# Gate logits of the first 16 token tiles as dot products on VectorE, VectorE in written order in layer 0's last part, and weight loads by guess

## The chip, the cores and the metric

The kernel runs on one core of a Trainium2 chip. The metric is the device time of one execution in microseconds (us); a kernel's time is the median over its runs. The engines are TensorE (PE; its weight loads are listed as PEld), VectorE (DVE), ScalarE (ACT), GpSimd (POOL) and SyncE (SP), which here issues most of the DMA loads.

## The reference, cut to what matters

Two layers work on x of 2708 tokens by 256 features, with an adjacency matrix `adj` (2708 x 2708, about 1.2% ones). Each is an attention over neighbours, then a mixture of 8 experts. What the change touches is layer 0:

```python
# layer 0, attention
h = layernorm(x)
q, k, v = h @ Wq.T + bq, h @ Wk.T + bk, h @ Wv.T + bv
s = where(adj > 0, q @ k.T / sqrt(256), -9e15)
x = x + elu(softmax(s, axis=-1) @ v)
# layer 0, experts: 8 experts, the 2 best of each token
xt = layernorm(x)
logits = xt @ Wr + br                      # the gate: 256 -> 8
weights, top_idx = two best of softmax(logits), divided by their sum
xn = (xt - mean(xt)) * rsqrt(var(xt) + 1e-5)
for e in range(8):                          # hidden size 1024
    h_e = gelu((xn * ln_g[e] + ln_b[e]) @ W1[e] + b1[e])
    y_e = h_e @ W2[e] + b2[e]
x = x + sum over the two chosen experts of weights * y_e
```

Layer 1 has the same frame: an attention whose score is a sum of a source and a destination term, and experts of hidden size 512.

## The kernel before

**Tiles.** The tokens form 22 tiles of up to 128 (the last has 20 rows). As queries they are taken in six blocks: five of 512 (four tiles each) and a last one of 148 (two tiles, 20 and 21). Blocks are numbered 0 to 5.

**Attention of layer 0.** For each block the kernel goes through the 22 key tiles. For a key tile it makes `scores` (L545 two matmuls per half of the features into PSUM, L557 the exponential on ScalarE, L560 a VectorE operation that takes the minimum with a large number and multiplies by the mask). Three key tiles later (`LAG`) `attend` (L609) multiplies the masked exponentials with the values into four PSUM accumulators, one for each query tile. The last two key tiles (from `KEYS` = 20 on) lie in columns of `adj` that are treated apart: one more matmul with `apart` (L552) makes the score of non-neighbours hugely negative, and a VectorE comparison writes the mask. `apart` is loaded and compared by `load_apart` (the comparison is L432): at key tile 14 of each block, at key tile 0 in the last.

**Masks.** While block b is computed, `masks_of(b + 1)` makes the next block's masks step by step: loads of `adj` into a ring of three buffers, 20 conversions to one byte (L411) and 20 transposes of four-byte words (L417), both on VectorE.

**Routing.** When a block's accumulators are complete, `evict` copies them out and puts one generator per tile into a `Line`. At each key tile `line.step()` starts the next waiting generator if at least `gap` = 3 steps have passed since the last one, and moves all running generators one step. A generator is `finish` (the division by the sum, elu, addition of x) and then `Experts.route`: statistics (L251 to L257, with a power on GpSimd in L257), two normalisations (L261; `xt` for the gate, and the row for the expert, which is normalised twice), two transposes of `xt` on TensorE (L274) and their copy on ScalarE (L275), the gate matmuls (L1156), the bias, the two best, two small matmuls that count how many earlier tokens chose each expert (L1188, L1189), and two indirect DMA writes on GpSimd (L1207) that put the row into the list of each of its experts, in DRAM. Tiles 0 to 3 are so routed during block 1, and so on; tiles 16 to 19 during block 5 and after it.

**Experts of layer 0.** At key tile 5 of block 5, `open` makes a ring of four tiles for expert weights (1.15 MB each), and `begin` cuts the lists as they are after 16 tiles into chunks of 128 rows (`place`), then starts the row loads of three chunks (SP, L1387 and L1393) and the weight loads of three chunks (GpSimd, indirect, L1368; a row index far outside means that nothing is loaded, which is used where a ring tile already holds the expert). `run` goes through 45 chunks, called slots, in written code and through the rest in conditional code. A slot turns its rows (`turned`: VectorE, L1429 a transpose in blocks, L1435 scale and shift), multiplies up (L1457) with the GELU on ScalarE (L1465), and down (L1473); VectorE weights the result (`y`, L1479), and an indirect DMA adds it to the tokens.

**Order.** SP's queue is in written order in the whole kernel. In layer 0, TensorE, VectorE, ScalarE and GpSimd are ordered by a scheduler when the program is built; `issue_after(self.issued.ins)` keeps some VectorE work of the experts behind a given instruction. Layer 1's attention and experts have TensorE, ScalarE and VectorE in written order.

## Time and profile before

| | |
|---|---|
| runs of the kernel before | 1213.34, 1210.01, 1208.46 us; median 1210.01 |
| the profiled execution | 1217.16 us, of which the span of the profile is 1215.5 us |
| instructions | 20794 |
| busy: TensorE matmuls, its weight loads | 1145.4 us (94%), 924.1 us (76%) |
| busy: VectorE, ScalarE, GpSimd | 566.2 us (47%), 431.9 us (36%), 416.0 us (34%) |
| mean granted clock of TensorE | 0.982 of full speed |
| DMA | 197.11 MB, 162 GB/s in the mean |

An L and a number name the line of the kernel's file from which an instruction comes. A group of instructions is written as output<-inputs with the partitions and elements of one instruction; a duration is the time of one instruction on its engine, and since neighbours overlap at their ends, the time from one start to the next is often shorter. "Waits" put an engine's idle time down to the instruction of another engine that came last. The granted clock is the share of its full speed at which TensorE ran in a stretch. The span is measured in one execution, and the difference of 1.7 us to that execution's time lies around it.

### The profile page before, as it was taken

How to read it: one execution, taken by the hardware profiler on the slowest of the kernel's cores; microseconds unless marked ns; L12 is line 12 of the kernel's file. 1: busy time of each engine (PE TensorE's matmuls, PEld its weight loads, DVE VectorE, ACT ScalarE, POOL GpSimd, SP SyncE). 2: the span in 40 equal slices, each digit the busy share in tenths (PEclk: the TensorE clock that was granted, in tenths of full speed). 3: DMA queues.
4: the chain of work that ended last, by engine and by line, in shares of the span. 5: the costliest groups of instructions: out<-in, count | busy, mean ns of one | idle time of the engine just before them, and what ended most of it. 6: DMA issues, size and time to landing. Idle time of an engine off the chain costs nothing. (4 is left out here: it accounts for less than half of the span.)

```text
span 1215.5 us, 20794 instructions
## 1 busy us (share of the span) xinstructions
PE 1145.4 (94%) x6512; PEld 924.1 (76%) x6512; DVE 566.2 (47%) x2147; ACT 431.9 (36%) x1252; POOL 416.0 (34%) x519
## 2 busy tenths in 40 slices
PE   8989999999998999999999999998999988899990
PEld 5666666666665666789999999996999977789880
DVE  5466663754645647452222222224866776322224
ACT  3222221221212222353333333333776747444440
POOL 3011021110211213253333343334645558555540
PEclk9999999999998999899999999999999999999996
DMA  9394962999969394847677955633002427555557
GB/s 200 58 181 76 194 160 88 226 209 267 221 133 219 83 192 164 276 102 219 174 222 228 352 118 154 179 95 100 1 1 76 178 62 209 168 139 132 170 179 282
DMA packets 199628, 197.11 MB, mean 162 GB/s; under 512 B 91403, under 2 KB 183012, under 8 KB 193368
## 3 DMA queue, kind: packets, MB, share of 16 engines
q1 hardware_dynamic: 172442, 109.39, 40.6%
q0 software_dynamic: 26176, 83.56, 21.8%
q10 hardware_dynamic: 894, 2.77, 0.6%
q8 instruction: 54, 0.88, 0.3%
q14 instruction: 62, 0.51, 0.1%
HBM read 252.62 MB, written 66.15 MB: 262 GB/s over the span
## 5 line engine op out<-in xcount | busy, mean ns | idle before, releaser
L1457 PEld LDWEIGHTS mm<-xe,ring 128*128 128x128 f32 x2192 | 259.7, 194 | 26.0 <-issue 11.7
L1457 PE MATMUL mm<-xe,ring 128*128 128x128 f32 x2192 | 265.6, 278 | 14.5 <-DMA ring<-L_ffn_packed,weight_row 7.1
L1473 PE MATMUL acc<-ring,hT 128*128 128x256 f32 x1096 | 254.3, 381 | 1.1 <-issue 1.1
L1465 ACT ACTIVATE hT<-mm,ring 128x128 f32<-128x128 f32 x548 | 156.6, 370 | 273.1 <-issue 168.1
L1473 PEld LDWEIGHTS acc<-ring,hT 128*128 128x128 f32 x1096 | 201.3, 191 | 26.0 <-issue 2.3
L609 PEld LDWEIGHTS acc<-v,p 128*128 128x128 f32 (+1 forms) x880 | 159.7, 190 | 65.2 <-issue 41.0
L609 PE MATMUL acc<-v,p 128*128 128x257 f32 (+1 forms) x880 | 204.6, 384 | 2.3 <-DVE p L560 1.3
L545 PE MATMUL s<-g,xnT 128*128 128x512 f32 x420 | 203.0, 603 | 0.0
L1479 DVE SCALAR_TENSOR_TENSOR y<-acc,who,bias 128x256 f32<-128x256 f32 x92 | 44.4, 482 | 339.2 <-PE acc L1473 322.9
L257 POOL TENSOR_TENSOR ln_rs<-ln_rs,minus_half 128x2 f32<-128x2 f32 x88 | 66.0, 752 | 252.0 <-DVE ln_rs L253 214.4
L1207 POOL DMA_INDIRECT disp<-row,to x88 | 90.4, 1027 | 166.2 <-DVE to L1204 58.2
L1368 POOL DMA_INDIRECT ring<-L_ffn_packed,weight_row x92 | 97.6, 1060 | 128.3 <-PE acc L1473 88.4
L557 ACT ACTIVATE p<-s 128x512 f32<-128x512 f32 x105 | 62.5, 596 | 181.4 <-PE s L545 143.0
L854 PE MATMUL acc<-parts,m 128*128 128x266 f32 x924 | 126.2, 293 | 0.0
L854 PEld LDWEIGHTS acc<-parts,m 128*128 128x128 f32 x924 | 117.1, 185 | 4.1 <-ACT raw L881 0.9
L545 PEld LDWEIGHTS s<-g,xnT 128*128 128x128 f32 x420 | 76.6, 192 | 53.8 <-issue 50.5
L560 DVE SCALAR_TENSOR_TENSOR p<-p,mT 128x512 f32<-128x512 f32 x100 | 68.4, 686 | 95.2 <-ACT p L557 93.6
L1492 POOL DMA_INDIRECT xd<-y,who x45 | 71.8, 1595 | 118.7 <-issue 70.4
L821 ACT CAST m<-mT 128x512 fp32r<-128x512 fp8e4 (+4 forms) x168 | 71.6, 475 | 11.4 <-PE acc L854 7.0
L1485 POOL DMA_INDIRECT xd<-y,who x47 | 47.1, 1002 | 23.6 <-issue 11.0
L411 DVE TENSOR_SCALAR m_rows<-adj 128x512 fp8e4<-128x512 int32 (+1 forms) x105 | 42.1, 432 | 2.0 <-DMA adj<-in_adj_dram 1.9
L417 DVE STREAM_TRANSPOSE mT<-m_rows 128x128 int32<-128x128 int32 x100 | 33.4, 393 | 0.1
(252 smaller groups left out, 1028.3 us busy)
## 6 DMA issues: line engine op xcount, KB each, us to landing
adj<-in_adj_dram SPq DMA_DIRECT2D x100, 256.0 KB
L_ffn_packed<-in_L_ffn_W_dram SPq DMA_DIRECT2D x16, 1024.0 KB
xg<-disp SPq DMA_DIRECT2D x368, 32.0 KB
L_ffn_packed<-in_L_ffn_W_dram SPq DMA_DIRECT2D x16, 512.0 KB
neighbours<-mT SPq DMA_DIRECT2D x5, 1408.0 KB
mT<-neighbours SPq DMA_DIRECT2D x5, 1408.0 KB
xin<-in_x_dram SPq DMA_DIRECT2D x42, 128.0 KB
ring<-L_ffn_packed SPq DMA_DIRECT2D x4, 1154.0 KB
```

The source lines that it names most:

```text
L257: nc.gpsimd.tensor_tensor(rs[:r, 1], rs[:r, 0], minus_half[:r], ALU.pow)
L545: nc.tensor.matmul(ps[:kr, :nb], xnT[:, c, k0 : k0 + kr], g[:, c, :nb], start=(c == 0), stop=(c == DC - 1 and k < KEYS),)
L560: nc.vector.scalar_tensor_tensor(p, p, LARGEST, mask, op0=ALU.min, op1=ALU.mult)
L609: nc.tensor.matmul(accs[j][:r], p[keys, q0 : q0 + r], v[keys, k, :], start=(k == 0), stop=(k == NT - 1),)
L821: nc.scalar.copy(m[:, : q1 - q0], MASKS[b].of_key(mTs[b], k)[:, q0 - b * BN : q1 - b * BN],)
L854: nc.tensor.matmul(acc[:r], masks[t], parts[:, k, i], start=(k == 0 and i == 0), stop=False,)
L1207: nc.gpsimd.indirect_dma_start(disp[:], bass.IndirectOffsetOnAxis(ap=to[:r, j : j + 1], axis=0), rows2[:r, j], None,)
L1368: nc.gpsimd.indirect_dma_start(w, None, packed[:], bass.IndirectOffsetOnAxis(ap=self.weight_row[:, s : s + 1], axis=0), bounds_check=E * P ...
L1457: nc.tensor.matmul(ps[:, i, :], w[:, c * hidden + f * P : c * hidden + (f + 1) * P], xe[:, c, :], start=(c == 0), stop=(c == DC - 1),)
L1465: nc.scalar.activation(hT[:, f, :], ps[:, i, :], AF.Gelu, bias=w[:, b1 + f : b1 + f + 1])
L1473: nc.tensor.matmul(ps, hT[:, f, :], w[:, w2 + f * D : w2 + (f + 1) * D], start=(f == 0), stop=(f == hc - 1),)
L1492: start = nc.gpsimd.indirect_dma_start(xd[:], at, y, None, bounds_check=N - 1, oob_is_err=False, compute_op=ALU.add)
```

## The change

The diff has six parts. Line numbers change; a name says which line is meant.

1. *Gate by dot products.* `gate_rows` copies the gate's weights Wr to all 128 partitions, subtracts each expert's mean over the features and leaves them as `wr_rows` (8 rows of 256 in each partition). It runs once, in block 0 at key tile 18, with one of the three `adj` buffers as the place for the raw weights. `gate_dots` computes the eight logits of a tile as eight VectorE operations that multiply two 128 x 256 tensors and sum along the row: four in `route`'s first step, four in its second. The result is multiplied by the row's factor `once` and the bias is added. That holds for tiles 0 to 15 (`t < self.early`), which then have no normalised `xt`, no transposes and no gate matmuls. Tiles 16 to 21 keep the matmuls; their transposed copy now takes a `raw` buffer.
2. *The far columns.* `load_apart` only loads now, at key tile 4 of blocks 0 to 4, and for block 5 at key tile 18 of block 4; `compare_apart` makes the comparison where `load_apart` stood.
3. *Written order.* From the start of block 5 until the experts of layer 0 end, VectorE's instructions are in written order. In block 5 a tile's generator starts four steps after the one before (`line.gap = GROUP`).
4. *The ring by guess.* At key tile 5 of block 5 the first three ring tiles are loaded by SP with the weights of experts 0, 1 and 3, before it is known which experts the first slots need. `place` compares the guess with the experts found, and the indirect loads bring only what differs. The steps of `begin` (chunk lists, row loads, weight loads) are spread: six at key tile 5, one each at 12, 16 and 20.
5. *Rows turned a slot ahead.* `turned(s + 1)` is written after `up(s)` in layer 0 too; `issue_after` is gone.
6. *Buffers.* The pool `fold` is replaced by one buffer of the masks' ring; some tiles of `fold_gate` (layer 1's gate, made in block 1) come from another pool.

```diff
-    def fold_gate():
+    def fold_gate(pool):
+        wdst_b = pool.tile([P, D], F32, name="wdst_b", bufs=1)
+        nc.sync.dma_start(wdst_b, a["L1_gnn_w_att"][D : 2 * D].partition_broadcast(P))
         for c in range(DC):
-            junk = small.tile([P, D], F32, name="junk", bufs=1)
+            junk = pool.tile([P, D], F32, name="junk", bufs=1)
             nc.vector.scalar_tensor_tensor(
...
             )
-        share = routing.tile([P, DC, P], F32, name="gT", bufs=2)
+        share = pool.tile([P, DC, P], F32, name="gT", bufs=2)
         nc.gpsimd.memset(share[:, 0], 1.0 / D)
...
+    def gate_rows(raw):
+        raw = raw.rearrange("p (d e) -> p d e", e=E)
+        mean = small.tile([P, E], F32, name="gate_mean", bufs=1)
+        nc.vector.tensor_reduce(mean, raw.rearrange("p d e -> p e d"), AX.X, ALU.add)
+        nc.vector.tensor_scalar(mean, mean, 1.0 / D, None, ALU.mult)
+        nc.gpsimd.tensor_tensor(
+            wr_rows, raw.rearrange("p d e -> p e d"),
+            mean.unsqueeze(2).to_broadcast([P, E, D]), ALU.subtract,
+        )
+    def gate_dots(lg, x, r, experts, unused):
+        for e in experts:
+            nc.vector.scalar_tensor_tensor(
+                unused, x, 1.0, wr_rows[:r, e],
+                op0=ALU.mult, op1=ALU.mult, accum_out=lg[:r, e : e + 1],
+            )
...
                         nc.sync.dma_start(adj[: ROWS[t], j], rest[j * P : j * P + ROWS[t]])
-                nc.vector.tensor_scalar(
-                    apart, adj[:, :n], 0, None, ALU.is_le, saturate=False
-                )
+                return apart, adj[:, :n]
+            def compare_apart(apart, adj):
+                nc.vector.tensor_scalar(apart, adj, 0, None, ALU.is_le, saturate=False)
                 return apart
...
-            with tc.tile_pool(name="fold", bufs=1, side="right") as fold:
-                wq = load_dmajor(fold, "L0_gnn_Wq", D)
-                wk = load_dmajor(fold, "L0_gnn_Wk", D)
+            fold = wide.tile([P, MASKS[0].width], FP8, name="mT", bufs=3)
+            fold = fold[:, : 16 * DC * D].bitcast(F32).rearrange("p (i c n) -> p i c n", i=4, c=DC)
+            if True:
+                wq = load_dmajor(fold[:, 0], "L0_gnn_Wq")
+                wk = load_dmajor(fold[:, 1], "L0_gnn_Wk")
                 load_x(0)
                 load_x(1)
-                wv = load_dmajor(wide, "L0_gnn_Wv", D)
+                wv = load_dmajor(wide.tile([P, DC, D], F32, name="wv"), "L0_gnn_Wv")
                 for t in range(2, 9):
...
                     raw = rows.tile([P, VALUES + 1], F32, name="raw", bufs=6)
-                    copied = (nc.scalar.copy if j % 2 else nc.vector.tensor_copy)(
+                    (nc.scalar.copy if j % 2 else nc.vector.tensor_copy)(
                         raw[: ROWS[t], : D + 1], accs[j][: ROWS[t]]
                     )
-                    if j == 0:
-                        experts0.issued = copied
                     line.add(finish(t, raw, total))
...
             late, total, accs, apart = [], None, None, None
-            folding = fold_gate()
+            folding = fold_gate(wide)
             for b, (b0, nb, ts_) in enumerate(BLOCKS):
                 later_mask = iter(())
+                if b == last:
+                    line.gap = GROUP
+                    order0.enter_context(
+                        tc.manual_schedule(engines={mybir.EngineType.DVE})
+                    )
                 if b + 1 < len(BLOCKS):
...
                         load_x(ts_[j])
+                    if b < last and k == GROUP:
+                        apart_adj = load_apart(b)
                     if k == (0 if b == last else NT - 8):
-                        apart = load_apart(b)
+                        apart = compare_apart(*apart_adj)
+                    if b == last - 1 and k == NT - 4:
+                        apart_adj = load_apart(last)
                     late.append((b, k, scores(b, k, g, apart, mT)))
...
                         total = all_sum(wide, sums, wv, D, "total0")
+                    if b == 0 and k == NT - 4:
+                        raw = wide.tile([P, BN // QUARTER, P], I32, name="adj", bufs=3)
+                        raw = raw.rearrange("p n e -> p (n e)").bitcast(F32)
+                        nc.sync.dma_start(
+                            raw, a["L0_ffn_Wr"].rearrange("d e -> (d e)").partition_broadcast(P)
+                        )
+                        gate_rows(raw)
                     if k == NT - 6 and b + 1 < len(BLOCKS):
...
                     if b == last and k == LAG + 2:
-                        experts0.open()
-                        for _ in experts0.begin():
-                            pass
+                        n = FULL_AFTER[experts0.early]
+                        guess0 = experts0.open(
+                            [i * (n // RING) * E // (n + GROUP) for i in range(AHEAD)] + [-1]
+                        )
+                        for _ in range(AHEAD):
+                            next(guess0)
+                        begin0 = experts0.begin()
+                        for _ in range(6):
+                            next(begin0)
+                    if b == last and k in (LAG + 7, LAG + 11, LAG + 15):
+                        next(begin0)
                 nc.sync.dma_start(neighbours[b][:], mT)
...
             own_norm, xd, disp, seen = self.own_norm, self.xd, self.disp, self.seen
-            w_gate, gate_bias = self.w_gate, self.gate_bias
+            gate_bias = self.gate_bias
             r = ROWS[t]
...
             mean, once, twice, _ = norm_stats(x[:r], r)
+            lg = small.tile([P, E], F32, name="lg")
+            by_dots = own_norm and t < self.early
+            if by_dots:
+                dots = small.tile([P, E], F32, name="dots")
+                gate_dots(dots, x[:r], r, range(E // 2), rows2[:r, 1, :D])
+                logits = dots[:r]
             yield
...
             if own_norm:
-                xt = rows.tile([P, D], F32, name="xn", bufs=4)[:r]
-                normed(xt, x[:r], mean, once)
                 normed(by_quarters(rows2[:r, 0, :D]), in_chunks(x[:r]), mean, twice)
+                if not by_dots:
+                    xt = rows.tile([P, D], F32, name="xn", bufs=4)[:r]
+                    normed(xt, x[:r], mean, once)
             else:
...
             if own_norm:
+                if by_dots:
+                    gate_dots(dots, x[:r], r, range(E // 2, E), rows2[:r, 1, :D])
                 nc.vector.tensor_copy(rows2[:r, 1, :D], rows2[:r, 0, :D])
...
                 )
-            lg = small.tile([P, E], F32, name="lg")
             if logits is None:
-                gT = routing.tile([P, DC, P], F32, name="gT", bufs=2)
+                gT = rows.tile([P, VALUES + 1], F32, name="raw", bufs=6)
+                gT = gT[:, :D].rearrange("p (c n) -> p c n", c=DC)
                 to_columns(gT[:, :, :r], xt, r)
...
                     nc.tensor.matmul(
-                        ps[:r, :E], gT[:, c, :r], w_gate[:, c, :],
+                        ps[:r, :E], gT[:, c, :r], wr[:, c, :],
                         start=(c == 0), stop=(c == DC - 1),
...
             self.weights = []
+            if self.own_norm:
+                yield
             for s in range(AHEAD):
...
-                nc.scalar.copy(self.ring[i][:, :1], pace()[:, :1])
+                if pace:
+                    nc.scalar.copy(self.ring[i][:, :1], pace()[:, :1])
                 nc.sync.dma_start(self.ring[i], self.packed_weights[0][e * P : (e + 1) * P, :])
...
                 raw = two.tile([P, DC, P], F32, name="xe_raw") if own_norm else xe
-                with tc.issue_after(self.issued.ins) if own_norm and s < often else ExitStack():
-                    nc.vector.transpose(
-                        raw.rearrange("p c (t i) -> p t c i", t=GROUP),
-                        xg.rearrange("p t (c j) -> p t c j", c=DC),
-                    )
+                nc.vector.transpose(
+                    raw.rearrange("p c (t i) -> p t c i", t=GROUP),
+                    xg.rearrange("p t (c j) -> p t c j", c=DC),
+                )
                 if own_norm:
...
-            def up(w, xe, factor, gated):
+            def up(w, xe, factor):
...
                 if own_norm:
-                    with tc.issue_after(self.issued.ins) if gated else ExitStack():
-                        nc.vector.tensor_scalar(bias2, w[:, b2:b1], factor, None, ALU.mult)
+                    nc.vector.tensor_scalar(bias2, w[:, b2:b1], factor, None, ALU.mult)
                 else:
...
                 w, (_, who) = self.weights[s], self.rows_[s]
-                if own_norm:
-                    xe = turned(s)
                 after = turned(1) if s == 0 and not own_norm else None
-                hT, bias2 = up(w, xe, who[:, 1:2], own_norm and s < 2)
-                if s + 1 < s1 and not own_norm:
+                hT, bias2 = up(w, xe, who[:, 1:2])
+                if s + 1 < s1:
                     xe = after or turned(s + 1)
...
                 nonlocal behind, xe
-                if not own_norm:
-                    xe = turned(s0)
+                xe = turned(s0)
                 for s in range(s0, s1):
...
         experts0.run(line)
+        order0.close()
         early_rows.close()
...
```

More of the change, by code (lines that the diff above doesn't have):

```diff
@@ L188, in adj_ffn_kernel, with load_dmajor @@
     bfc_b = load_bcast("L1_gnn_b_fc", D)
-    wdst_b = load_bcast("L1_gnn_w_att", D, D)
-    def load_dmajor(pool, name, n):
-        t = pool.tile([P, DC, n], F32, name=f"{name}_w")
+    def load_dmajor(t, name):
         nc.sync.dma_start(t, a[name].rearrange("(c p) n -> p c n", p=P))
@@ L197, in adj_ffn_kernel @@
     wr = const.tile([P, DC, E], F32, name="wr")
+    wr_rows = rows0.tile([P, E, D], F32, name="wr_rows", bufs=1)
     wg = const.tile([P, DC, E], F32, name="wg")
@@ L229, in times_gate @@
         def times_gate(dst, src):
-            turned = routing.tile([P, DC, P], F32, name="gT", bufs=2)
+            turned = pool.tile([P, DC, P], F32, name="gT", bufs=2)
             to_columns(turned, src, P)
@@ L498, in layer0_attention @@
                 for w in (wq, wk):
-                    f = fold.tile([P, DC, D], F32, name=f"flat{len(flat)}")
+                    f = fold[:, 2 + len(flat)]
                     for o in range(DC):
@@ L1038, in adj_ffn_kernel, with __init__ @@
     class Experts:
-        def __init__(self, layer, hidden, packed_weights, w_gate, gate_bias, own_norm, xd, disp, early):
+        def __init__(self, layer, hidden, packed_weights, gate_bias, own_norm, xd, disp, early):
             self.hidden, self.packed_weights, self.own_norm = hidden, packed_weights, own_norm
-            self.w_gate, self.gate_bias, self.xd, self.disp = w_gate, gate_bias, xd, disp
+            self.gate_bias, self.xd, self.disp = gate_bias, xd, disp
             self.seen = const.tile([P, E], BF16, name=f"seen{layer}")
@@ L1478, in down @@
                 y = two.tile([P, D], F32, name="y", bufs=3)
-                self.issued = nc.vector.scalar_tensor_tensor(
+                nc.vector.scalar_tensor_tensor(
                     y, ps, who[:, 1:2], bias2, op0=ALU.mult, op1=ALU.add
@@ L1585, in adj_ffn_kernel @@
     packed1 = pack_weights("L1_ffn", 512, False)
-    experts0 = Experts(0, 1024, packed0, wr, br_b, True, xd0, disps[0], 16)
-    experts1 = Experts(1, 512, packed1, wg, gb_b, False, xd1, disps[1], 14)
+    experts0 = Experts(0, 1024, packed0, br_b, True, xd0, disps[0], 16)
+    experts1 = Experts(1, 512, packed1, gb_b, False, xd1, disps[1], 14)
     neighbours = [
@@ L1592, in adj_ffn_kernel @@
     line = Line(3)
+    order0 = ExitStack()
     layer0_attention(line)
```

## The prediction

> **What bounds the kernel now.** I read the page first, then TensorE's waits, the timeline at its longest stall, and the groups by shape. TensorE's row says who is full:
>
> ```profile
> PE 1145.4 (94%) x6512; PEld 924.1 (76%) x6512; DVE 566.2 (47%) x2147; ACT 431.9 (36%) x1252; POOL 416.0 (34%) x519
> ```
>
> A saved microsecond of TensorE work counts wherever TensorE doesn't wait. Layer 0's attention fills 0 to 501 us, its experts 502 to 829. The waits of TensorE up to 550 us (us in total, times, longest) add up to under 18 us:
>
> ```profile
> PE misc L466 <- ACT xnT L275: 3.2, 6, 0.7
> PE s L552 <- DVE apart L432: 3.0, 1, 3.0
> PE misc L274 <- DVE xn L261: 2.7, 6, 0.8
> PE acc L609 <- DVE p L560: 1.3, 1, 1.3
> ```
>
> The second is the one long stall. Its cost doesn't end with the 3.0 us; in the table of stretches the granted clock (after the counts) falls behind it:
>
> ```profile
> 370.00:375.00 5.00, 2.53 (x12) 1.88 (x10) 5.00 (x15) 0.00 (x0) 3.24 (x4) 1.00 1.12 197
> 375.00:380.00 5.00, 3.97 (x13) 2.24 (x14) 1.39 (x4) 0.77 (x2) 0.18 (x1) 0.55 1.07 274
> 380.00:385.00 5.00, 5.00 (x13) 2.66 (x12) 1.36 (x2) 1.20 (x2) 0.00 (x0) 0.77 0.98 338
> 500.00:505.00 5.00, 4.02 (x19) 3.48 (x19) 3.25 (x12) 0.74 (x2) 0.00 (x0) 0.68 0.93 323
> 505.00:510.00 5.00, 5.00 (x31) 4.89 (x31) 3.36 (x24) 3.07 (x9) 0.00 (x0) 0.64 0.52 169
> ```
>
> 0.55 and 0.77 over 10 us mean half clock for 6.8 us; the last two rows say the same at the experts' start. What gate logits cost TensorE is read from starts in its timeline:
>
> ```profile
> 225.89 1.90 PE L609 MATMUL acc<-v,p 128*128 128x257 f32 x8
> 227.62 0.38 PE L274 MATMUL misc<-ident,xn 128*128 128x128 f32 x2
> 227.84 1.88 PE L545 MATMUL s<-g,xnT 128*128 128x512 f32 x4
> 229.56 1.90 PE L609 MATMUL acc<-v,p 128*128 128x257 f32 x8
> 231.29 0.51 PE L1156 MATMUL misc<-wr,gT 128*128 128x8 f32 x4
> 231.66 1.96 PE L545 MATMUL s<-g,xnT 128*128 128x512 f32 x4
> 233.46 1.90 PE L609 MATMUL acc<-v,p 128*128 128x257 f32 x8
> ```
>
> One key tile is 1.73 (scores) + 1.72 (attend) = 3.45 us. The transposes add 0.22; the gate matmuls 0.37, and the scores after them last 1.80 instead of 1.72. One tile's gate: 0.67 us.
>
> **The Trainium skill.** "TensorE: Matmul & The Clock Gate", What's actually happening: one idle window of about 3.4 us halves the clock until a busy window has passed. The trace agrees: 3.02 us idle, then 6.8 us (two such windows) at half; it also shows 2.5 us idle enough at 836 and 1 us at 500, where the matmuls before were narrow. "SBUF — State Buffer", SBUF: two separate sides: a VectorE operation with two SBUF inputs and a GpSimd operation reading SBUF exclude each other. The dots have two such inputs; no row of this trace isolates that price.
>
> **Part 1, dots instead of matmuls.** Removed: 16 tiles (0 to 15, routed in blocks 1 to 4) x 0.67 = 10.7 us of TensorE, 16 ScalarE copies, 16 VectorE normalisations. Added: 128 dots. The nearest row is L212, the same shape with an accumulator (starts at 36.0 and 36.5, before anything competes):
>
> ```profile
> L212 DVE SCALAR_TENSOR_TENSOR junk<-wfc,L_gnn_w_att_b x2: 417/420/424, 36.0 to 36.5; 128x256 f32<-128x256 f32 x2
> L212 DVE DVE_READ_ACCUMULATOR junk<-wfc,L_gnn_w_att_b x2: 81/82/82, 36.3 to 36.8; 128x1 f32 x2
> ```
>
> "VectorE: DVE Perf Modes", the errata section, gives (N+151)/0.96 ns for fp32 with two tensors: 424 ns at 256, as here. Operations overlap at their ends: from the start of one dot to the next's is 0.457, to another operation's 0.35. I take 0.41; ends 0.35 and 0.46. 128 x 0.41 = 52 us, less 16 x 0.33 of normalisation: +47 us of VectorE over 335 us.
>
> Does it reach TensorE? The changed program's order gives the VectorE work between one mask multiply and the next; priced start to start (mask multiply 0.60, conversion 0.335, word transpose 0.24, 256-wide operations 0.20 to 0.40, narrow ones 0.08) block 1's key tiles 3 to 13 cost 3.5, 4.3, 3.7, 3.4, 4.0, 4.5, 3.4, 4.1, 3.5, 4.1, 3.4 = 41.9 us against 11 x 3.45 = 38.0. VectorE ends 3.9 us behind (5.4 at 0.46 a dot). The attend stands three key tiles after its scores: 10.35 us, less about 1.5 for exponential and multiply, leaves 8.85. So nothing is lost in block 1; block 2 ends 2.6 behind, block 3 at most 4.4. Only in block 4 are two tiles bunched after key tile 14: 11.6 us of VectorE before the next multiply, and TensorE's order wants the first tile's selection (L1188 now) 9.5 us after those scores, while VectorE gives it after 1.4 + 8.9 + 0.5 = 10.8. With the smaller waits that follow: -2 us. Filling the rows of weights (a reduction, 5.5 us on GpSimd if L764's 0.74 us for 256 is scaled by 8, a 1 MB broadcast) lies at block 0's end, where the DMA engines idle (105 to 120 us) and nothing needs it for four key tiles; it borrows one of three adjacency buffers, of which the mask loads have that slack.
>
> **Part 2, the far-column comparison (L432) split from its load.** Before, it stood behind eight conversions and eight transposes. Now, in block 3, after the last multiply come four of each: 4 x 0.335 + 4 x 0.24 + 0.34 + 0.36 = 3.0, plus 1.4 = 4.4 us after scores 19; TensorE arrives after 3 x 1.73 = 5.2. In block 4 it is ready 4 us early. The stall goes: +3.0 and half of 6.8 us of clock, together +6.4. The loads move on SP: one 0.3 MB load in small pieces now competes in block 0 at key tile 4, where the DMA share is 1.2: -1 (0 to -2).
>
> **Part 3, the last block in written order.** From TensorE's last comparison of block 4 to the end of attention took 452.8 to 500.7 = 47.9 us, 44.5 when the two attends (3.4) that the new order puts earlier are taken off. Following both queues: VectorE gives tile 15's selection and the first multiply about 11.0 us after that comparison, TensorE wants it at 9.7 (-1.3); then TensorE's queue has tile 16's transposes behind half an attend, and they wait for exponential, addition, statistics, the GpSimd power (0.75) and the normalisation in one chain until 17.1, TensorE being there at 14.1 (-3.0); later waits 2.5, TensorE's slack being used up. The end comes at 49.3, so -4.8. In this lie 1.3 us of gates of tiles 18 and 19, which before stood among the experts.
>
> **Part 4, the experts' start.** Before, slot 0 began at 501.7 and slot 5 at 542.7: 41.0 us for five slots of 7.03 (35.2), so 5.8 lost to four tiles' gates, half clock and inputs coming late (on SP, `xg` loads sat in a queue full of GpSimd's ring loads from 490 to 506). Now the ring's three direct loads (3 x 1.15 MB) are on SP at key tile 5, and from the reference's inputs the full chunks per expert after 16 tiles are 4, 4, 3, 4, 4, 3, 3, 4: slots 0, 1, 2 belong to experts 0, 1, 3, the guess, so GpSimd's three loads are skipped. Turned rows are ready a slot ahead. Left: two gates 1.3 and one half-clock window 1.7: 3.0, gain +2.8 (0 to +4.5). Queued behind the fills on SP are the row loads; they have 25 us. Steady slots don't change: TensorE has no gap there. VectorE's y now stands behind the next slot's turning, which has 7 us to spare. Layer 1's own order is unchanged.
>
> **Sum.** 10.7 + 6.4 + 2.8 - 2 - 4.8 - 1 = 12.1 us: the span 1215.5 becomes 1203.4. The profiled execution took 1217.2, 7 above the median of 1210.0; I move the median by the same: 1198.
>
> **Rivals.** (a) VectorE nowhere reaches TensorE in the last block and the experts start at full clock: 10.7 + 6.4 + 4.5 - 1.3 = 20, 1190. For it: TensorE waited for VectorE's multiply only 1.3 us before. Against: the chain of tile 16 is in written order. (b) Gains eaten: stalls of 1 to 3 us in blocks 1, 2 and 4, and the 3.0 us stall of part 3 falling into one clock window (-1.7 each): 1203 to 1209. For it: eleven key tiles in a row have more VectorE work than TensorE work. (c) Slower: VectorE becomes the bound in blocks 1 to 4, because a dot interleaved with GpSimd costs more than L212's. Block 1's lag is 3.9 + 32 x (price - 0.41), and TensorE stalls by what exceeds 8.85, four times; the 12 us are gone at 0.66 us a dot, and at 0.8 the four blocks lose 30, which gives 1228. Against it: L624, also two inputs, means 0.416 among GpSimd's work. (d) The guess doing nothing changes part 4 by at most its 2.8.
>
> **Chances.** Forecast 0.54 (its own range 1192 to 1204), (a) 0.10, (b) 0.21, (c) 0.15. About 0.5%, 6 us, is what can be told from no change here. Faster: forecast, (a) and a quarter of (b), 0.69; same 0.15; slower 0.16. The range 1188 to 1212 leaves out most of (c) and the lower tail of (a).
>
> **What would show it.** Right: 32 transposes gone from L274 and the gate matmuls down to six tiles; no 3 us gap before the comparison in block 3; TensorE gapless in blocks 1 and 2; small gaps near key tile 17 of block 4 and tile 16's transposes; slot 5 under 39 us after slot 0. Wrong: many gaps before attends ended by VectorE, dots above 0.5 us start to start, half-clock windows in blocks 1 to 4, or later mask conversions waiting for adjacency loads.

## The result and the profile after

The changed kernel takes 1230.3 us (median of six runs, 1227.1 to 1231.4), the kernel before 1210.7 us in the same comparison: a ratio of 1.0155 (95% interval 1.0137 to 1.0174). It is 19 us slower; 12 us faster was forecast. Its profiled execution took 1230.8 us, with a span of 1229.1.

The page's row of busy times after the change says that TensorE does less, as it should (96 matmul records and 6 us fewer), and VectorE 55 us more:

```profile
PE 1139.2 (93%) x6416; PEld 919.0 (75%) x6416; DVE 621.2 (51%) x2389; ACT 423.9 (34%) x1234; POOL 422.6 (34%) x524
```

So the loss is waiting. TensorE's waits over the whole changed kernel (us in total, times, longest) show where; the far-column stall of block 3 is gone from the list, and a six times longer one has come:

```profile
PE acc L632 <- DVE p_last L583: 21.3, 4, 17.9
PE mm L1512 <- DMA ring<-L_ffn_packed,weight_row: 8.9, 5, 3.1
PE misc L1242 <- DVE sel L1237: 5.1, 4, 2.1
```

The landmarks place it. They are the starts of the first matmul of a kind in the timeline, the end of the last attend, and the start of the last of 45 `y` of layer 0's written slots, all in us:

| | before | changed | difference |
|---|---|---|---|
| block 5 begins (first `g_last` scores) | 457.2 | 443.8 | -13.4 |
| attention ends | 500.7 | 521.0 | block 5: +33.7 |
| experts begin (first L1457, now L1512) | 501.7 | 522.7 | |
| `y` of slot 9 | 583.4 | 598.6 | from the attention's end: -5.0 |
| `y` of slot 44 | 826.1 | 841.8 | from slot 9: +0.4 |
| end of the span | 1215.5 | 1229.1 | from slot 44: -2.0 |

Up to block 5 and from the experts on the change does what was forecast, or more. Block 5, the smallest block, takes 77.2 us instead of 43.5. Its stretches (busy time of PE, PEld, DVE, ACT, POOL, then granted clock, DMA share and GB/s) are of the changed kernel:

```profile
445.00:450.00 5.00, 5.00 (x36) 4.15 (x35) 4.22 (x21) 1.47 (x5) 0.83 (x1) 1.00 1.00 237
450.00:455.00 5.00, 0.74 (x6) 0.46 (x5) 2.67 (x18) 0.83 (x4) 1.03 (x1) 0.79 1.07 225
455.00:460.00 5.00, 0.00 (x0) 0.00 (x0) 0.00 (x0) 0.00 (x0) 0.99 (x2) 0.50 1.18 155
460.00:465.00 5.00, 0.00 (x0) 0.00 (x0) 0.00 (x0) 0.00 (x0) 0.00 (x0) 0.50 1.08 200
465.00:470.00 5.00, 0.00 (x0) 0.00 (x0) 0.21 (x1) 0.00 (x0) 0.00 (x0) 0.50 0.71 168
470.00:475.00 5.00, 4.53 (x9) 1.58 (x10) 4.50 (x17) 0.79 (x3) 0.00 (x0) 0.50 1.09 245
```

From 455 to 469 the engines stand still, but for two short GpSimd instructions, while the DMA engines are full or nearly so (a share of 1.18, 1.08 and 0.71). VectorE's timeline names what it waits for (start, duration, instruction, and in brackets idle time before it with its releaser):

```profile
453.01 0.17 DVE L1258 TENSOR_REDUCE to<-hot 128x2 int32<-128x16 f32 x1
469.79 0.32 DVE L455 TENSOR_SCALAR apart_last<-adj_rest 128x296 fp8e4<-128x296 int32 x1 [16.61 <-DMA adj_rest<-in_adj_dram]
470.02 0.75 DVE L583 SCALAR_TENSOR_TENSOR p_last<-p_last,mT_last 128x148 f32<-128x148 f32 x3
```

This is the comparison of the last block's far columns (part 2). TensorE needs its result only at key tile 20. But VectorE is now in written order (part 3), the comparison is written at key tile 0, and three mask multiplies that TensorE does need are queued behind it. The Trainium skill, "Perfetto Trace Analysis", Tensor Engine Instruction, calls VectorE's queue "strict FIFO", first in, first out. The trace agrees: these multiplies, whose exponentials were finished, stood for 16.6 us behind the comparison.

Why is the load so late? SP's timeline: block 4's far columns are issued at 412.1, the next instruction waits until 436.5, and the last block's far columns follow at 462.1.

```profile
412.13 0.62 SPq L447 DMA_DIRECT2D adj_rest<-in_adj_dram  x1
436.54 0.32 SPq L418 DMA_DIRECT2D adj<-in_adj_dram  x1
...
460.86 1.13 SPq L397 DMA_DIRECT2D xin<-in_x_dram  x2
462.09 0.78 SPq L451 DMA_DIRECT2D adj_rest<-in_adj_dram  x2
```

SP waits 23.7 us for a GpSimd memset of an adjacency buffer (L410), and that one for VectorE's mask conversion (L431), which frees the buffer. SP's waits, then GpSimd's timeline:

```profile
SPq L418 <- POOL adj L410: 24.1, 2, 23.7
```

```profile
435.87 0.65 POOL L410 MEMSET adj<- 128x640 int32 x1 [4.25 <-DVE m_rows L431]
```

From 436.5 SP needs 25.6 us more to reach the last block's far columns (7.9 us of it in waits for weight copies, `L_ffn_packed`, to land), and these have landed at 469.8, 7.7 us after their issue. In the changed kernel VectorE makes the conversion only after all 20 mask multiplies of block 4; the kernel before did it after the tenth:

```profile
435.31 0.49 DVE L431 TENSOR_SCALAR m_rows<-adj 128x640 fp8e4<-128x640 int32 x1 [0.21 <-issue]
```

```profile
412.50 0.49 DVE L411 TENSOR_SCALAR m_rows<-adj 128x640 fp8e4<-128x640 int32 x1
```

(The first is of the changed kernel, the second of the kernel before: the first of the last block's five conversions.) VectorE wasn't busy until then: from 382 to 412 it idled 2.8 us before most mask multiplies. So it isn't lack of time but the scheduler's order that puts the routing of block 3's tiles and the conversions late.

So there are three candidates for the cause: written order (part 3), dots (part 1) and the early far-column loads (part 2).

### The profile page after: what moved, and what is told of

The parts are those of the page before. It is cut to its first block, busy times and chain, and to the rows that moved or that the text cites. A ratio compares the mean times of both kernels' runs of the same rounds, so it can differ in the third digit from the quotient of the medians.

```text
span 1229.1 us, 20855 instructions
## 1 busy us (share of the span) xinstructions
PE 1139.2 (93%) x6416; PEld 919.0 (75%) x6416; DVE 621.2 (51%) x2389; ACT 423.9 (34%) x1234; POOL 422.6 (34%) x524
## 5 line engine op out<-in xcount | busy, mean ns | idle before, releaser
L1512 PEld LDWEIGHTS mm<-xe,ring 128*128 128x128 f32 x2192 | 260.9, 194 | 21.8 <-issue 12.2
L1512 PE MATMUL mm<-xe,ring 128*128 128x128 f32 x2192 | 264.1, 278 | 13.7 <-DMA ring<-L_ffn_packed,weight_row 8.9
L583 DVE SCALAR_TENSOR_TENSOR p<-p,mT 128x512 f32<-128x512 f32 x100 | 72.6, 728 | 76.3 <-ACT p L580 76.2
L1540 POOL DMA_INDIRECT xd<-y,who x47 | 46.9, 998 | 26.2 <-DVE y L1534 13.5
L261 DVE SCALAR_TENSOR_TENSOR row<-x,wr_rows 128x256 f32<-128x256 f32 x128 | 52.4, 418 | 0.4
L632 PE MATMUL acc<-v,p_last 128*128 128x257 f32 (+3 forms) x88 | 31.7, 468 | 21.4 <-DVE p_last L583 21.3
```

The source lines that it names most:

```text
L583: nc.vector.scalar_tensor_tensor(p, p, LARGEST, mask, op0=ALU.min, op1=ALU.mult)
L632: nc.tensor.matmul(accs[j][:r], p[keys, q0 : q0 + r], v[keys, k, :], start=(k == 0), stop=(k == NT - 1),)
L1512: nc.tensor.matmul(ps[:, i, :], w[:, c * hidden + f * P : c * hidden + (f + 1) * P], xe[:, c, :], start=(c == 0), stop=(c == DC - 1),)
```

## The experiments

In the four sets the kernel before took 1211 to 1218 us, so each ratio is to the kernel before in its own set. A time that was expected in us is on the scale of the first comparison, where 1.01 is 12 us. The landmarks in the table are us of each one's profile.

| run | ratio (95% interval) | block 5 begins | attention ends | experts begin | slot 44 |
|---|---|---|---|---|---|
| before | 1 | 457.2 | 500.7 | 501.7 | 826.1 |
| changed | 1.0155 (1.0137 to 1.0174) | 443.8 | 521.0 | 522.7 | 841.8 |
| e2: part 3 undone | 1.0075 (1.0057 to 1.0093) | 443.2 | 487.8 | 517.0 | 837.7 |
| e3: last load early | 1.0114 (1.0091 to 1.0136) | 443.5 | 517.0 | 519.1 | 839.7 |
| e4: part 1 undone | 1.0138 (1.0085 to 1.0192) | 458.3 | 520.9 | 522.8 | 845.6 |
| e5: part 1 alone | 1.0061 (1.0039 to 1.0082) | 445.8 | 498.4 | 510.1 | 833.1 |
| e6: part 2 undone | 1.0040 (1.0029 to 1.0051) | 447.8 | 506.7 | 508.6 | 828.8 |
| e7: part 2 alone | 1.0167 (1.0129 to 1.0204) | 462.4 | 508.6 | 527.6 | 848.6 |
| e8: load at key tile 12 | 0.9996 (0.9977 to 1.0014) | 447.4 | 500.7 | 502.7 | 822.0 |
| e9: e8, scheduler order | 0.9988 (0.9973 to 1.0003) | 447.3 | 494.3 | 503.4 | 824.2 |
| e10: written order from block 4 | 1.0008 (0.9987 to 1.0029) | 451.9 | 504.9 | 506.0 | 826.6 |
| e11: from block 1 | 1.0121 (1.0094 to 1.0148) | 470.9 | 520.9 | 523.0 | 844.0 |
| e12: e10 without guess | 1.0083 (1.0055 to 1.0112) | 455.0 | 505.1 | 514.2 | 836.8 |
| e13: e8, order for the experts alone | 0.9960 (0.9944 to 0.9975) | 447.5 | 492.4 | 497.0 | 817.7 |
| e14: e13, block 3 in order too | 0.9895 (0.9871 to 0.9919) | 443.0 | 487.5 | 492.1 | 813.9 |

### First set: which part

**Part 3 undone (e2).**

```diff
-                    order0.enter_context(
-                        tc.manual_schedule(engines={mybir.EngineType.DVE})
-                    )
```

> The changed kernel without its third part: VectorE in the last block is ordered by the scheduler again, all else as changed. My theory: the 17.9 us wait of TensorE for the first masked p_last comes from written order, which puts the far-column comparison of the last block (its load landed at 469.8 us) ahead of the first mask multiply. Then the wait goes, and with it half clock and small waits: the last block (first scores to last attend, 77.2 us in the changed kernel, 43.5 before) takes 44 to 50 us and the median 1198 to 1206. Rival, the dots (or the transfers) are late for every order: the wait stays over 8 us and the median over 1218.

The block is short again, 44.6 us, as expected. The time isn't: the ratio falls from 1.0155 to 1.0075 only, half of the loss and the rival's figure (over 1218 us), and the experts begin 29 us after the attention's end. TensorE's waits have a new longest one, at the last tiles' routing:

```profile
PE misc L294 <- DVE xn L281: 25.5, 6, 14.5
```

The loads are as late as before (far columns at 461.9, rows of tile 16 at 460.8). Scheduler order moves the place where the lateness is paid and about halves its price. My theory that written order by itself makes the loss fell here.

**Early load for the last block (e3).**

```diff
-                adj = wide.tile([P, GROUP, REST], I32, name="adj_rest", bufs=1)
+                adj = wide.tile([P, GROUP, REST], I32, name="adj_rest" if b < last else "adj_rest_last", bufs=1)
...
                     if b < last and k == GROUP:
                         apart_adj = load_apart(b)
+                        if b == last - 1:
+                            last_adj = load_apart(last)
+                    if b == last and k == 0:
+                        apart_adj = last_adj
                     if k == (0 if b == last else NT - 8):
                         apart = compare_apart(*apart_adj)
-                    if b == last - 1 and k == NT - 4:
-                        apart_adj = load_apart(last)
```

> The changed kernel, but the last block's far columns have a buffer of their own and are loaded at key tile 4 of block 4, 14 key tiles earlier; written order and the comparison's place are kept. My theory: the late load alone makes the long wait; the comparison finds its data, the wait of 17.9 us goes, the last block takes 48 to 56 us and the median is 1202 to 1210. Rival, written order as such (place's 20 operations and tile 16's chain in line ahead of mask multiplies): the last block still takes over 60 us and the median stays over 1214.

The load is issued at 412.8, the comparison runs at 438.6 without a wait, and yet the block takes 73.4 us and the ratio is 1.0114. These are the rival's figures, and in part its mechanism: tile 16's chain and the chunk table stand in line ahead of mask multiplies. But what costs the time is what they wait for. VectorE's timeline shows two more late transfers of SP's queue: tile 16's rows of x, then the store of a mask (`neighbours`), which it names as what a copy for the chunk table waits for.

```profile
467.84 0.43 DVE L651 TENSOR_TENSOR x<-neg,xin 128x256 f32<-128x256 f32 x1 [10.40 <-DMA xin<-in_x_dram]
...
477.98 0.17 DVE L1286 COPY n_e<-misc 128x8 f32<-128x8 f32 x1 [6.77 <-DMA neighbours<-mT]
```

Not one load is late but the whole of SP's queue.

**Part 1 undone (e4).**

```diff
-            by_dots = own_norm and t < self.early
+            by_dots = False
```

> The changed kernel without dots: all tiles use the gate matmuls as before; the weights' rows are still filled. Theory that the bunched dots of block 4 hold the mask conversions back, those the adjacency buffers, those SP's queue (23.7 us behind one memset), and that queue the far columns' load: without dots the load is issued near 449 us and lands near 456, the wait is under 3 us; TensorE has its 10.7 us of gates again, and the median is 1205 to 1214. Rival, the load is late because of the transfers ahead of it on SP whatever VectorE does: the wait stays over 10 us and the median is over 1225.

The last block's first conversion comes at 438.2, the far columns are issued at 467.0, VectorE waits 11.5 us for them and TensorE 8.7. The wait is neither under 3 nor, for TensorE, over 10 us, and the ratio of 1.0138 is the rival's. The theory of the dots fell: the bunch is there without them. (SP's wait behind memsets L410 is even longer in sum, 34.1 us in two.)

**Part 1 alone (e5).** The kernel before with the dots, their rows and the buffers of part 6; everything else as before.

> The kernel before with the first and the last part alone: dots for 16 tiles, rows filled in block 0, buffers as changed; comparison behind its load at the old place, scheduler order, no guess, turning at the slot's start. By the terms of my sum: 10.7 us of TensorE less 2 for the bunch of block 4, and the stall of the far columns in block 3 stays (or moves with the schedule): 1200 to 1204. Rival, dots delay the masks and through them the loads: later waits of TensorE take over half of the gain, 1206 or more.

Here the conversions stand where they stood (408.5 to 425.6), and block 5 begins 11.4 us earlier than before. But it ends only 2.3 us earlier, and the experts begin 8.4 us later. VectorE waits 9.9 us in two waits for far columns, TensorE 4.0 us in block 5 with 13.7 us at half clock. After it, VectorE waits 4.7 us for the first slots' rows, which land at 508:

```profile
508.41 0.45 DVE L1471 STREAM_TRANSPOSE xe_raw<-xg 128x256 f32<-128x256 f32 x1 [4.72 <-DMA xg<-disp]
```

So the trace reads that what TensorE gains in blocks 1 to 4 is given back as soon as it has to wait for loads that don't come earlier with it; no run tests this by itself. My figure was missed and the rival's (1206 or more) was met, but not in its way: the masks aren't late.

### Second set: part 2

The orders of the programs had by now shown a pattern: the bunch is in every kernel with the far-column load at key tile 4, and in none without.

**Part 2 undone (e6).**

```diff
-                    if b < last and k == GROUP:
-                        apart_adj = load_apart(b)
                     if k == (0 if b == last else NT - 8):
-                        apart = compare_apart(*apart_adj)
-                    if b == last - 1 and k == NT - 4:
-                        apart_adj = load_apart(last)
+                        apart = compare_apart(*load_apart(b))
```

> The changed kernel without its second part: load and comparison of the far columns stand together at the old places, all else as changed. My theory now: the load at key tile 4 is what makes the scheduler put block 4's routing and the last block's mask conversions 8 to 10 key tiles later, and with them SP's queue. Then the conversions are back at some 408 to 426 us and the tokens' rows (xin) for tiles 16 to 19 are issued near 440 us, not 460. But the comparison in written order still waits for a load issued at the last block's start: a wait of 4 to 10 us for p_last. Time 0 to 12 us above the kernel before, well below the changed kernel's 19. Rival, the dots or the written order make SP late: the rows stay near 460 us and the time within 3 us of the changed kernel.

As expected, and at 1.0040: conversions from 410.4, rows of tile 16 at 440.4, and a wait of 7.3 us for `p_last`, since the last comparison in written order now waits 14.2 us for its load.

**Part 2 alone (e7).** The kernel before with the lines that e6 takes out.

> The kernel before with the second part alone: loads of the far columns at key tile 4 (and 18 for the last block), comparisons at the old places, scheduler order. My theory: the 3.0 us stall of block 3 is gone, yet the conversions of the last block come after 435 us, the rows for tiles 16 to 19 after 458 us, the experts begin after 512 us (501.7 before), and the kernel is 8 to 25 us slower than before. Rival, the split is harmless or good by itself (my forecast gave it 6.4 us of gain): not slower than before, and the experts begin before 500 us.

This one edit makes the kernel before 1.7% slower, as much as the whole change. Its first conversion of the last block is at 437.8 (412.5 before), rows of tile 16 are issued at 463.7 (438.7 before), and TensorE's waits from 457 to 530 us are headed by the experts' start:

```profile
437.76 0.49 DVE L411 TENSOR_SCALAR m_rows<-adj 128x640 fp8e4<-128x640 int32 x1
```

```profile
PE mm L1462 <- DVE xe L1440: 18.9, 1, 18.9
PE misc L274 <- DVE xn L261: 5.3, 1, 5.3
```

**The load at key tile 12 (e8), and in scheduler order (e9).**

```diff
-                    if b < last and k == GROUP:
+                    if b < last and k == 12:
```

> The changed kernel with one number changed: the far columns of blocks 0 to 4 are loaded at key tile 12 instead of 4 (compared at 14 as before), the last block's at key tile 18 of block 4 as changed. In the program's order the conversions of the last block then stand after 10 to 16 multiplies of block 4, as before the change, not after all 20. My theory: SP is on time, the last block's load lands before 450 us, the wait of 17.9 us is gone, and the time is 5 to 25 us below the changed kernel's (1196 to 1215 on the first chip's scale). Rival, the written order alone costs the last block its time: still over 60 us for the last block and within 5 us of the changed kernel.

> As the kernel before this one in the list (load at key tile 12), with VectorE in scheduler order in the last block and layer 0's experts. If written order costs the last block something even with its data there (my forecast: 4.8 us), this one is 1 to 6 us faster; if it is what makes the experts' start quick (rows turned a slot ahead of need), it is slower by 1 to 6 us.

One number takes away the 19 us. In e8 the conversions come at 410.0 to 427.5, and the last block's comparison is done within 0.9 us of block 5's start (447.4):

```profile
409.99 0.49 DVE L431 TENSOR_SCALAR m_rows<-adj 128x640 fp8e4<-128x640 int32 x1
...
447.96 0.31 DVE L455 TENSOR_SCALAR apart_last<-adj_rest 128x296 fp8e4<-128x296 int32 x1 [3.39 <-DMA adj_rest<-in_adj_dram]
```

So part 2's early load is the cause, by the order that the scheduler makes of it. Why its order changes so (no wait on the chip asks for it) no run here shows. But both kernels are equal to the kernel before, and 12 us had been forecast; e9's ratio is 0.0008 below e8's, within the intervals, so neither of its two expectations is shown. Three things are left: the stall of block 3 is back in both (2.9 us), e8's block 5 takes 53.3 us, and in e9 the experts begin 9.1 us after the attention's end, TensorE being idle for 7.9 of them, while VectorE works on tiles 20 and 21 ahead of the first slot's rows. What written order loses in the block it wins at the experts' start, so the two are equal.

### Third set: written order elsewhere, the guess, the baseline

**Written order from block 4 (e10) and from block 1 (e11).** In e10 `b == last` becomes `b == last - 1` ahead of `order0.enter_context`, in e11 `b == 1`; the load is at key tile 4.

> The changed kernel with VectorE's written order beginning one block earlier, at block 4 (loads at key tile 4 as changed). Block 4's routing and the last block's conversions then stand at their written places (conversions after 3 to 7 multiplies, not after 20). My theory: the split itself is good once the order of block 4 is fixed: no stall in block 3, no late SP queue; block 5 begins near 441 us, the last block takes 49 to 54 us, the experts begin within 3 us of the attention's end, and the kernel is 4 to 14 us faster than the kernel before. Rival, written order in block 4 has waits of its own (TensorE in block 4 over 80 us again): not faster than before.

> As the kernel above, with the written order from block 1 on. If written order costs a few tenths of a microsecond per tile in waits for ScalarE and GpSimd, blocks 1 to 3 lose 0 to 6 us against it; the time is 0 to 6 us above that of the kernel above. If the scheduler's order has hidden losses in these blocks too, it is up to 4 us below.

Both expectations missed; in e10 the rival came true, in e11 neither (1.1% above e10). In e10 block 4 begins at 362.1, 15.8 us ahead of the kernel before, and then takes 89.7 us. The longest of VectorE's waits there:

```profile
DVE m_rows L431 <- DMA adj<-in_adj_dram: 15.9, 1, 15.9
```

It is the same failure one block earlier: a conversion that isn't urgent waits for its load, with urgent multiplies behind it. But the conversions now come at 393 to 409 us with the load still at key tile 4, so the early load makes them late only through the scheduler's order. In e11 such waits add up to 46.1 us in blocks 1 to 4.

**Without the guess (e12).** As e10, with `experts0.open()` and no direct loads.

> As the first kernel of this list, without the guess: the first three weight loads (2.2 MB each, 5 us at the 420 GB/s seen there) are issued by GpSimd after the chunks are placed. If the experts' start is bound by these loads and the row loads behind them, they begin 3 to 8 us later and the time is 3 to 8 us above; if TensorE's own end bounds it (my forecast: at most 2.8), within 3 us.

The experts begin 9.1 us after the attention's end, not 1.1, and the ratio is 0.0075 higher, 9 us. VectorE's first turning of rows waits 8.1 us, which the trace puts down to a row load, while the DMA engines are full (a share of 1.05 from 505 to 510). The guess is worth about 8 us when the attention ends at 505 us.

**The kernel before once more.**

> The kernel before once more, for its profile: the first profiled execution took 1217.2 us against a median of 1210. If a stage was slow in that one execution by chance, a second profile shows which; I expect 1207 to 1214 and the same landmarks within 2 us up to the end of layer 0.

It took 1222.2 us, against the expected 1207 to 1214. All landmarks up to slot 44 lie within 0.6 us of the first profile; from there to the end it took 393.8 us, the first 389.3. So these two executions differ by 4.5 us behind slot 44 and hardly before it; where that comes from is not shown. Landmarks are therefore compared up to slot 44 only.

### Fourth set: the two losses left

**Written order for the experts alone (e13).** e8, with `order0.enter_context(...)` moved behind the last attends, ahead of the last `evict`.

> The changed kernel with the load at key tile 12 and VectorE's written order beginning only at the end of the attention (its last copies out of PSUM), so for the experts alone. If the two losses left are of order (written order in the last block: 53.3 us against 46.9 in scheduler order; the routing of tiles 20 and 21 ahead of the first slot's rows in scheduler order: 9 us of idle TensorE), both go: the last block takes 46 to 49 us, the experts begin within 3.5 us of its end, before 499 us, and the kernel is 4 to 9 us faster than before. Rival, the start is bound by the weight and row loads: the experts begin at 501 to 505 us as in the two kernels before it, and the time is within 2.5 us of the kernel before.

Block 5 takes 44.9 us, the experts begin 4.6 us after it (1.1 more than expected; 1.7 of it is a wait for rows), and the kernel is 0.40% faster than before.

**And block 3 from key tile 10 to its end (e14).**

```diff
+                    if b == 3 and k == 10:
+                        order1 = tc.manual_schedule(engines={mybir.EngineType.DVE})
+                        order1.__enter__()
...
+                if b == 3:
+                    order1.__exit__(None, None, None)
                 nc.sync.dma_start(neighbours[b][:], mT)
```

> As the kernel above, with VectorE in written order also in block 3 from key tile 10 to its end. The comparison then stands after 14 multiplies of block 3 with one conversion ahead of it, and the last block's conversions still after 6 to 12 multiplies of block 4. If the 3.0 us stall and its half clock can be had without the bunch of block 4, block 4 begins 4 to 7 us earlier and the time is 2 to 7 us below the kernel above. Rival, VectorE in written order waits for adjacency loads in block 3 (as it did in block 4): a new stall, no gain or a loss up to 8 us.

Block 4 begins 4.5 us earlier than in e13, block 5 too, and slot 44 comes 3.8 us earlier. The kernel is 1.05% faster than the kernel before (0.81% to 1.29%): it beats both. Against e13 the medians differ by 6.5 us (1200.5 and 1207.0), within the expected range; what lies beyond the 3.8 us isn't in layer 0's landmarks and stays open. TensorE's waits in blocks 3 and 4 (285 to 447 us) are, in e14,

```profile
PE s L568 <- ACT p L580: 1.0, 1, 1.0
PE acc L632 <- ACT p L580: 0.5, 1, 0.5
PE misc L1245 <- DVE sel L1240: 0.5, 1, 0.5
```

where e13 still has

```profile
PE s L575 <- DVE apart L455: 2.9, 1, 2.9
```

## Why the prediction was wrong, step by step

**The step that failed is in part 2: "The loads move on SP: one 0.3 MB load in small pieces now competes in block 0 at key tile 4, where the DMA share is 1.2: -1 (0 to -2)."** I priced the moved loads as traffic in block 0 and asked when each comparison would be ready for TensorE. I didn't ask what the move does to the order of everything else, nor followed the last block's load along SP's queue to its landing. The facts were at hand: the program's order shows the last block's five conversions behind all 20 multiplies of block 4. I saw half of it ("two tiles are bunched after key tile 14"), priced what TensorE waits for in block 4, -2, and stopped there. The right question was what is late next: conversions, then adjacency buffers, then SP, then all that SP carries. Where 1 us had been put down, it cost 19 us here (the changed kernel against e8) and 20 us alone (e7: 1.67% of 1211).

**Part 3** was worked out with the data there ("-4.8"), and that held neither way. In the changed kernel the block lost 33.7 us: 25.3 of idle TensorE, some 8 of work at half clock (half of 470.5 to 476.8 and of 487.0 to 497.3), 1.3 for two gates, less 2.1 for attends that its order puts ahead of block 5; about 1 us stays unassigned. With its data in time (e8) it lost 9.9: 4.4 of idle TensorE, 3.4 for 6.8 us at half clock, 1.3 for two gates. The forecast's own terms (waits of 1.3, 3.0 and 2.5, gates 1.3) add up to 8.1 and not to 4.8, and it doesn't say what it took off. The clock was missing from the sum; I had it only in a rival. In scheduler order the same block takes 44.9 us (e13): written order there has nothing to give.

**Part 1** was right. A dot takes 0.42 us, as the row of L212 said:

```profile
L261 DVE SCALAR_TENSOR_TENSOR row<-x,wr_rows x128: 381/420/428, 139.3 to 449.6; 128x256 f32<-128x256 f32 x128
```

Blocks 1 to 4 of e8 take 323.6 us against 332.9, so 9.3 less where 10.7 - 2 was forecast, and the changed kernel begins block 5 at 443.8, where my terms give 443.1. VectorE is no bound: rival (c) fell, and in blocks 1 to 4 of the changed kernel TensorE waits for it 1.4 us in all. (A side sum was off without harm: 0.74 us times 8 is 5.9, not 5.5, and filling the weights' rows took GpSimd 4.7 us.) What fell is the premise "a saved microsecond of TensorE work counts wherever TensorE doesn't wait": in e5 TensorE reaches block 5 11.4 us earlier, and the kernel is 7 us slower.

**The stall in block 3** was nearly right: e14 against e13 gains 4.5 where I had 6.4. The size was off because the clock stood at half for 3.4 us after it in e8, not for 6.8.

**Part 4** had the right sign and was too small: -5.0 us from the attention's end to slot 9, for 2.8. By its own measure, from slot 0 to slot 5, it forecast 38.2 us after 41.0, and the changed kernel takes 33.5. It rested on a wrong size, "3 x 1.15 MB", which the description of the kernel before gives too: four loads of 1154 KB in the page before are of layer 1's ring. The page of the changed kernel says of layer 0's

```profile
ring<-L_ffn_packed SPq DMA_DIRECT2D x3, 2182.0 KB
```

Rival (d), a guess that matters by at most 2.8, is refuted: 8 us in e12. That the loads are twice as large fits this, but no run varies their size.

**The rivals.** The result lies on the slower side, for which I had one mechanism, VectorE as the bound, and that wasn't it. None of the rivals was a late transfer behind a full queue, though it was the failure that part 3 invites. The nearest was the last sign of being wrong, "later mask conversions waiting for adjacency loads"; in the changed kernel it is the other way round, the loads wait for the conversions. That e14 reaches 0.9895, which is 1198 us on the scale of the median before, is no proof of the forecast: its terms differ (no written order in block 5, a larger gain at the experts' start).

## What to carry to other kernels

When a load is moved, follow it to its landing in every queue it passes, and then compare the whole program's order, not only the instructions edited: a scheduler may answer with a new order elsewhere, and the first instruction to look at is the one that frees a buffer for a transfer. Written order is dear where a patient instruction that waits for a transfer stands ahead of urgent ones, and not free where the data is there (block 5 took 53.3 us in e8, 46.9 in e9); put it on the stretch that needs it. If several late stalls go and the time doesn't, suspect that they all hang on one queue.

## What the runs showed of the hardware that was not expected

- Half clock followed 1.7 us of idle time. In e8 TensorE waited twice for `p_last`, 0.64 and 1.06 us within the 3 us up to 490, and then ran 6.8 us at half clock (490.5 to 497.3). The Trainium skill, "TensorE: Matmul & The Clock Gate", What's actually happening, speaks of one idle window of about 3.4 us. Both this and the 3.02 us of the stall in block 3, which the prediction took as agreeing, are less than that. What decides in such a case no run here isolates.

```profile
487.68 1.24 PE L632 MATMUL acc<-v,p_last 128*128 128x257 f32 x4 [0.64 <-DVE p_last L583]
489.98 1.69 PE L632 MATMUL acc<-v,p_last 128*128 128x257 f32 x4 [1.06 <-DVE p_last L583]
```

- SP's queue was held by its own earlier large loads. In e9 the issues of one slot's four row loads (32 KB each) stretch over 15.7 us, against 1.8 us at other times. SP's waits from 466 to 490 us say why: two of the issues waited, 13.9 us in sum, until weight loads of 2.2 MB that SP had issued at 459.5 had landed. The changed kernel has the same two waits (16.0 us).

```profile
470.63 15.66 SPq L1441 DMA_DIRECT2D xg<-disp  x4
```

```profile
SPq L1441 <- DMA ring<-L_ffn_packed: 13.9, 2, 8.3
```
